# The opening of a fused attention and feed-forward kernel: first loads on two queues, both weight products before the keys, h1's copies on SyncE behind the keys

## The chip, the cores and the metric

One Trainium2 chip, one NeuronCore of it. The time is the device time of the whole program in microseconds (us), median of several runs. Engines are named as in the profile: PE is TensorE (PEld its weight loads), DVE is VectorE, ACT is ScalarE, POOL is GpSimd, SP is SyncE, which here issues DMAs only. ACT issues DMAs too, from the same instruction queue in which its activations stand.

## The reference

The input x has 2 batches of 2048 rows of 256 features, all in float32.

```python
xn = layernorm(x)                                   # over the 256 features, eps 1e-5
q, k, v = xn @ Wq, xn @ Wk, xn @ Wv                 # 256 -> 256
scores = where(causal, q @ k.T, -max) * 256 ** -0.5
attention = softmax(scores) @ v @ Wo
h = silu(tlin(xn, w1)) * tlin(xn, w2)               # 256 -> 1024; tlin(x, w) = (x @ w.T) * s
h = gelu(tlin(h, h1)); h = gelu(tlin(h, h2))        # 1024 -> 1024, exact gelu
return x + attention + tlin(h, w3)                  # 1024 -> 256
```

The entries of w1, w2, h1, h2 and w3 are -1, 0 or 1, each output feature with a scale s.

## The kernel before, in words

**Two parts.** The program first does all of attention, then the feed-forward part inside a branch (L1075): a flag, made during attention, tells whether the ternary weights have no low bits, and `ffn_ternary` (L692) runs then. Nothing of the feed-forward part starts before attention ends. It multiplies by h1 and h2 in seven products of quarters instead of eight, from sums of quarters that lie in the DRAM tensors `factors`.

**Numbers in two parts.** A float32 operand of a product is split into a high part, rounded for TensorE, and a low part, the rest. `hi_lo` (L207) does it: ACT copies the high part, DVE subtracts it. A product of two such operands is three matmuls: high by high, high by low, low by high. With the 256 features in two chunks this makes six matmuls of 512 columns.

**Weights.** Queries and keys never appear by themselves: `weights_product` (L212) makes wqk from Wq and Wk, so that a score is (xn wqk) xn, and wvo from Wv and Wo. What the code calls keys is the transposed, split xn; queries are xn times wqk, values xn times wvo.

**Blocks.** Rows come in blocks of 512 (TB), four a batch (NB), each of four tiles of 128 rows. Attention starts with the last block of the first batch, number 3. For each block, `start_keys` (L270) takes statistics on DVE (`stats`, L230), the root on ACT (`root`, L236) and normalises x in place on POOL (L278); `keys` (L288) transposes it on PE, splits it and stores it to DRAM (`xT_d`, L306, 1 MB a block, read again by the feed-forward part). `queries` (L308), `values` (L322) and `score` (L344) are PE's work on it. The second batch's keys are transposed by DVE in small squares and two passes through DRAM (`turn_blocks`, `fetch_blocks`), and so are the exponentials of most score rows: tile b goes to d in DRAM, and comes back as e. `turn` splits them (pT) and `weigh` (L429) multiplies them by the values.

**The opening** (L178 to L617): loads of x for blocks 3 to 0 on SP, of Wq and Wk on ACT; idle matmuls on PE (`WARM`); wqk; loads of Wv and Wo into the buffers that Wq and Wk leave; then keys, queries and one row of scores of block 3, wvo, and keys, scores and values of blocks 2 to 0.

**The loop after it** goes over 32 tiles of rows (j), and mixes the scores of tile j with the weighing of earlier tiles (`merged`, L43, by their numbers of columns). A tile is weighed no sooner than DELAY or DELAY_BLOCKS columns of PE work after its scores.

**Beside it**, from j = 3, `beside` (L595) counts PE's columns and each time a gap is full takes the next of a list of steps (`looks`): `fetched_weights` (L572) loads the next feed-forward weights on ACT's queue into two stg buffers; `low` and `odd` look at their bits on ACT and DVE; `sum_up` makes sums of h1's quarters on DVE and `store_sums` writes them to the DRAM tensor `factors["h1"]`; `copy_factors` (L538) fills the rest of it with three copies from DRAM to DRAM for each of four chunks, 256 KB each. At the end xh0 is loaded again (L690).

**Order on the engines.** Each engine works through its own list in order. The framework's scheduler builds these lists ahead of the run: it may put an instruction earlier than the text has it when its operands and its buffer are free. `tc.issue_after(ins)` puts what is made inside it behind `ins` on the engine of `ins`. The `marks` are the last such instructions: `marks["DVE"]` the last score row's copy, `marks["ACT"]` the last exponential. In the trace of before, the twelve copies of h1, which have no operand to wait for, are issued from ACT's queue between 1.7 and 19.6 us.

## Time and profile before

| what | value |
|---|---|
| time, median of 3 runs (lowest to highest) | 874.41 us (873.32 to 876.95) |
| the profiled execution's own time | 872.97 us |
| its span in the profile | 871.1 us |
| PE busy | 851.1 us (98%) |
| DVE, ACT, POOL busy | 630.3, 498.2, 236.3 us |
| DMA moved | 162.5 MB, 187 GB/s over the span |
| PE's first matmul of the feed-forward part | 278.16 us |
| mean granted PE clock | 0.993 |

Times inside the profile count from the start of its span; the profiled execution's own time is 1.9 us longer than the span. A row of a timeline gives start, duration, engine, line, operation and tiles (out from in), how many instructions were merged, and in brackets how long the engine was idle before it and what ended that. A row of a windows table gives the window, its length, busy time and instructions of PE, PEld, DVE, ACT and POOL, the granted PE clock, the DMA engines' busy share and GB/s. A row of waits gives engine and line, what it waited for, the sum in us, how many times, and the longest. A matmul's shown duration includes its way through the array, so that 512 columns show some 0.37 us while the next starts after 0.23; costs below are by such starts.

### The profile page before, as it was taken

To read this page: it belongs to the slowest core of one execution; us is meant where nothing else is said; L and a number is where in the kernel's file an instruction comes from. 1 tells how busy PE (TensorE), PEld (TensorE's weight loads), DVE (VectorE), ACT (ScalarE), POOL (GpSimd) and SP (SyncE) were. 2 spreads that over 40 slices of the span, in tenths; PEclk is the share of its full clock that TensorE was granted. 3 is DMA by queue.
4 is the path that set the end of the run, shared out by engine and by line. 5 is a ranking of instruction groups with operands and counts; after the bars stand their busy time and mean duration, and the time that the engine had idled before them with its cause. 6 is when DMAs were issued, how large, how long until landed. Compare 5 with 4: busy or idle time off the path is not lost.

```text
span 871.1 us, 12211 instructions
## 1 busy us (share of the span) xinstructions
PE 851.1 (98%) x4280; PEld 720.7 (83%) x4280; DVE 630.3 (72%) x1127; ACT 498.2 (57%) x881; POOL 236.3 (27%) x176
## 2 busy tenths in 40 slices
PE   8999999999989999999999999999999999999996
PEld 5888888988877878888988888988888898888886
DVE  5699688786873995985496596569478648848663
ACT  2547555755644665677266486536657635657670
POOL 4112633201111473540143150025024012402401
PEclk8999999999999999999999999999999999999999
DMA  9867599866792979743424444443444432144412
GB/s 322 312 230 226 176 326 300 298 230 212 243 324 93 375 280 336 273 146 143 139 87 150 146 144 145 149 127 103 145 145 145 146 139 97 49 145 146 145 49 77
DMA packets 63845, 162.51 MB, mean 187 GB/s; under 512 B 6560, under 2 KB 36384, under 8 KB 54560
## 3 DMA queue, kind: packets, MB, share of 16 engines
q1 hardware_dynamic: 58304, 145.92, 48.4%
q10 hardware_dynamic: 5472, 15.73, 5.6%
q8 instruction: 36, 0.59, 0.3%
q14 instruction: 33, 0.27, 0.1%
HBM read 120.21 MB, written 47.71 MB: 193 GB/s over the span
## 4 chain that ended last, share of the span: by engine, by line
PE 61%; DMA 3%; POOL 1%; DVE 1%; issue 0%; SPq 0%; DVEq 0%; POOLq 0%
PE ps_h_X L780 26%; PE ps_h_Z L780 13%; PE ps_w_B L736 10%; PE ps_h_Y L780 7%; PE ps_y L918 6%; DMA stgt_h<-in_ffn_h_w 1%; DMA w_h_S<-factors_h 1%; POOL sums_h L151 1%; DVE f_w_B L762 0%; DMA rt<-r_d 0%; POOL rt L908 0%; DVE h_B L720 0%; DMA out<-yt 0%; POOL f_w_B L761 0%; DVE f_w_B L742 0%
## 5 line engine op out<-in xcount | busy, mean ns | idle before, releaser
L359 PE MATMUL pss<-k,q 128*128 128x512 f32 (+3 forms) x480 | 110.4, 368 | 2.1 <-DVE q L210 1.1
L359 PEld LDWEIGHTS pss<-k,q 128*128 128x128 f32 x480 | 81.6, 189 | 14.9 <-DVE q L210 1.4
L780 PE MATMUL ps_h_X<-h_h_T,w_h_S 128*128 128x512 f32 x384 | 89.1, 389 | 0.3 <-DMA w_h_S<-factors_h 0.3
L780 PEld LDWEIGHTS ps_h_X<-h_h_T,w_h_S 128*128 128x128 f32 x384 | 72.0, 188 | 15.6 <-ACT k_h_u L801 0.7
L438 PE MATMUL po<-v,pT 128*128 128x512 f32 x272 | 79.0, 403 | 3.7 <-ACT pT L418 2.8
L420 POOL TENSOR_TENSOR pT<-e,pT 128x512 fp32r<-128x512 f32 (+3 forms) x30 | 35.6, 1188 | 161.6 <-ACT pT L418 111.0
L908 POOL TENSOR_TENSOR rt<-rt,xt 128x1024 f32<-128x1024 f32 x8 | 19.6, 2453 | 209.9 <-DMA rt<-r_d 209.9
L801 ACT ACTIVATE k_h_u<-k_h_u,h_s_sb 128x512 f32<-128x512 f32 x64 | 46.3, 724 | 41.1 <-DVE k_h_u L800 40.9
L741 ACT ACTIVATE f_w_B<-ps_w_B,w_s_sb 128x512 f32<-128x512 f32 x64 | 43.0, 684 | 43.5 <-PE ps_w_B L736 43.5
L918 PEld LDWEIGHTS ps_y<-w_sbt,h_h_B 128*128 128x128 f32 x512 | 62.0, 192 | 0.3
L918 PE MATMUL ps_y<-w_sbt,h_h_B 128*128 128x256 f32 x512 | 62.1, 283 | 0.0
L736 PE MATMUL ps_w_B<-xh,w_sb 128*128 128x512 f32 x256 | 59.5, 390 | 1.3 <-DVE r L457 1.3
L418 ACT CAST pT<-e 128x512 fp32r<-128x512 f32 (+3 forms) x60 | 32.6, 574 | 48.9 <-DMA e<-d 31.0
L780 PE MATMUL ps_h_X<-h_h_T,w_h_A 128*128 128x512 f32 x256 | 59.3, 389 | 0.0
L780 PE MATMUL ps_h_Y<-h_h_B,w_h_A 128*128 128x512 f32 x256 | 59.3, 389 | 0.0
L736 PE MATMUL ps_w_B<-xh1t,w_sb 128*128 128x512 f32 x256 | 58.7, 389 | 0.0
L438 PEld LDWEIGHTS po<-v,pT 128*128 128x128 f32 x272 | 48.6, 192 | 11.6 <-ACT pT L418 3.3
L736 PEld LDWEIGHTS ps_w_B<-xh,w_sb 128*128 128x128 f32 x256 | 47.8, 188 | 11.2 <-issue 1.5
L780 PEld LDWEIGHTS ps_h_Y<-h_h_B,w_h_A 128*128 128x128 f32 x256 | 48.0, 188 | 10.0
L780 PEld LDWEIGHTS ps_h_X<-h_h_T,w_h_A 128*128 128x128 f32 x256 | 48.0, 188 | 10.0
L736 PEld LDWEIGHTS ps_w_B<-xh1t,w_sb 128*128 128x128 f32 x256 | 48.0, 188 | 10.0
L380 ACT ACTIVATE s<-s,low 128x1024 f32<-128x1024 f32 (+7 forms) x48 | 43.0, 897 | 20.3 <-DVE low L374 19.9
(139 smaller groups left out, 1846.7 us busy)
## 6 DMA issues: line engine op xcount, KB each, us to landing
w_h_S<-factors_h SPq DMA_DIRECT2D x32, 1024.0 KB, 4.7
w_h_A<-factors_h SPq DMA_DIRECT2D x24, 1024.0 KB, 4.7
d<-b SPq DMA_DIRECT2D x18, 512.0 KB, 4.2
e<-d SPq DMA_DIRECT2D x72, 128.0 KB, 4.1
xT_d<-k SPq DMA_DIRECT2D x8, 1024.0 KB, 7.5
stg<-in_ffn_h_w ACTq DMA_DIRECT2D x16, 512.0 KB, 6.6
x<-in_attn_x SPq DMA_DIRECT2D x16, 256.0 KB, 5.5
r_d<-r SPq DMA_DIRECT2D x8, 512.0 KB, 5.3
```

What stands on the lines that cost most here:

```text
L151: engine.tensor_tensor(sums[:, i, :], x, y, op)
L359: nc.tensor.matmul(out=ps[:, :w], lhsT=qs[n][:, c, a, ts(t, P)], rhs=ks[m][:, c, b, :w], start=(k == 0), stop=(m < n and k == 3 * DC - 1),)
L380: marks["ACT"] = nc.scalar.activation(st["s"][:, at], st["s"][:, at], AF.Exp, bias=low, accum_out=st["sums"][:, u // UK : u // UK + 1],).ins
L418: nc.scalar.copy(hi, src)
L420: engine.tensor_tensor(lo, src, hi.bitcast(F32), ALU.subtract)
L438: nc.tensor.matmul(out=st["po"], lhsT=pT[:, 0, ts(j, P)], rhs=vs[m][:, j, :, :], start=(m == first and j == 0), stop=False,)
L736: nc.tensor.matmul(out=p, lhsT=w[:, c, ts(o, P)], rhs=xh[:, c, a, :], start=(c == 0 and a == 0), stop=(c == DC - 1 and a == 1),)
L741: nc.scalar.activation(f, p1, AF.Silu, scale=sc["w1"][:, o : o + 1])
L780: nc.tensor.matmul(out=out[o], lhsT=w[:, c, ts(o, P)], rhs=sets[right][c][:, a, :], start=(start and c == 0 and a == 0), stop=(c == HK - 1 ...
L801: nc.scalar.activation(C[k][o], r[o] if r else banks[o], AF.Gelu, scale=s[:, at : at + 1])
L908: nc.gpsimd.tensor_tensor(rest, rest, xt, ALU.add)
L918: nc.tensor.matmul(out=ys[t][:, :D], lhsT=h[c][:, a, ts(t, P)], rhs=w3_sb[:, c, :], start=(c == 0 and a == 0), stop=(c == HC - 1 and a == 1),)
```

## The change

- x of block 3 is fetched in two halves by SP and ACT. Wq and Wv go on SP's queue, Wk and Wo on ACT's, all ahead of blocks 2 to 0. Wv and Wo have a buffer of their own (a b buffer), so they wait for nothing.
- The idle matmuls have 256 columns instead of 512, and are 26 instead of 14; six more stand between keys and queries of block 3.
- Both weight products stand before the keys of block 3. Each has its matmuls in one PSUM tile, and its copies (`copied`) are made later: wqk's behind the keys, wvo's behind the scores of block 3 and queued behind the last high and low parts.
- Block 3's normalised x is made by POOL (tiles 0 and 2) and ACT (tiles 1 and 3). Statistics of blocks 2 to 0 are queued behind wqk's low part.
- Queries and scores do the six matmuls in another order: chunk inside, part outside.
- h1's copies go from ACT to SP, three behind each of the four xT_d stores of the first batch. The step of the list that held each triple is gone.
- Loads of feed-forward weights are queued behind the last exponential before them.

```diff
 TURN_KEYS = [8, 10, 12, 14]
 LOOKS_FROM = 3
 LEAD = 2
-WARM = 14
+WARM = 26
+WARM_KEYS = 6
...
         ps_o = actx.enter_context(tc.tile_pool(name="ps_o", bufs=2, space=PSUM))
         xs, rstds, ks, qs, vs = {}, {}, {}, {}, {}
-
-        def load_x(n):
+        marks = {}
+
+        def load_x(n, queues):
             t = xp.tile([P, NT, D], F32, tag="x", name=f"x_{n}")
-            for h in range(2):
+            for h, queue in enumerate(queues):
                 src = x[n // NB, ds((n % NB) * TB + h * 2 * P, 2 * P), :]
-                nc.sync.dma_start(out=t[:, ts(h, 2), :], in_=src.rearrange("(t p) d -> p t d", p=P))
+                queue.dma_start(out=t[:, ts(h, 2), :], in_=src.rearrange("(t p) d -> p t d", p=P))
             return t
-        xs[NB - 1] = load_x(NB - 1)
-        raw = {}
-        for name, src in (("q", wqT), ("k", wkT)):
-            raw[name] = stgp.tile([P, DC, D], F32, tag="stg", name=f"raw_{name}")
-            nc.scalar.dma_start(out=raw[name], in_=src)
+
+        xs[NB - 1] = load_x(NB - 1, (nc.sync, nc.scalar))
+        raw = {name: stgp.tile([P, DC, D], F32, tag="stg", name=f"raw_{name}") for name in "qk"}
+        both = bp.tile([P, 2, DC, D], F32, tag="b", name="raw_vo")
+        raw["v"], raw["o"] = both[:, 0], both[:, 1]
+        for name, src, queue in (
+            ("q", wqT, nc.sync), ("k", wkT, nc.scalar), ("v", wvT, nc.sync), ("o", wo, nc.scalar)
+        ):
+            queue.dma_start(out=raw[name], in_=src)
         nc.scalar.preload_act_table(AF.Sqrt)
         for n in range(NB - 2, -1, -1):
-            xs[n] = load_x(n)
+            xs[n] = load_x(n, (nc.sync, nc.sync))
         ident = cp.tile([P, P], F32, name="ident")
         make_identity(nc, ident)
...
         nc.gpsimd.memset(ones, 1.0)
-        idle = sp.tile([P, S], F32, tag="s", name="idle")[:, : TB // 2].bitcast(BF16)
+        idle = sp.tile([P, S], F32, tag="s", name="idle")[:, : TB // 4].bitcast(BF16)
         nc.vector.memset(idle, 0.0)
         ps_idle = ps_s.tile([P, TB], F32, tag="ps", name="ps_idle")
-        for _ in range(WARM):
-            nc.tensor.matmul(out=ps_idle, lhsT=idle[:, :P], rhs=idle, start=True, stop=True)
+
+        def keep_warm(k):
+            for _ in range(k):
+                nc.tensor.matmul(
+                    out=ps_idle[:, : TB // 2], lhsT=idle[:, :P], rhs=idle[:, : TB // 2], start=True, stop=True
+                )
+
+        keep_warm(WARM)
         def hi_lo(hi, lo, src):
-            nc.scalar.copy(hi, src)
-            nc.vector.tensor_tensor(lo, src, hi.bitcast(F32), ALU.subtract)
+            marks["hi"] = nc.scalar.copy(hi, src).ins
+            marks["lo"] = nc.vector.tensor_tensor(lo, src, hi.bitcast(F32), ALU.subtract).ins
         def weights_product(name, aT, b, factor):
             r = cp.tile([P, DC, 2, D], F32R, name=name)
+            ps = ps_s.tile([P, DC, D], F32, tag="ps", name=f"ps_{name}")
             for c in range(DC):
-                ps = ps_s.tile([P, TB], F32, tag="ps", name=f"ps_{name}_{c}")
                 for d in range(DC):
                     nc.tensor.matmul(
-                        out=ps[:, :D], lhsT=aT[:, d, ts(c, P)], rhs=b[:, d, :],
+                        out=ps[:, c, :], lhsT=aT[:, d, ts(c, P)], rhs=b[:, d, :],
                         start=(d == 0), stop=(d == DC - 1),
                     )
-                f = rp.tile([P, D], F32, tag="y", name=f"wf_{name}_{c}")
-                nc.scalar.mul(f, ps[:, :D], factor)
-                nc.vector.tensor_copy(r[:, c, 0, :], f)
-                nc.vector.tensor_tensor(
-                    r[:, c, 1, :], f, r[:, c, 0, :].bitcast(F32), ALU.subtract
-                )
-            return r
+
+            def copied():
+                f = rp.tile([P, NT, D], F32, tag="r", name=f"wf_{name}")[:, :DC, :]
+                nc.scalar.mul(f, ps, factor)
+                nc.vector.tensor_copy(r[:, :, 0, :], f)
+                marks["lo"] = nc.vector.tensor_tensor(
+                    r[:, :, 1, :], f, r[:, :, 0, :].bitcast(F32), ALU.subtract
+                ).ins
+
+            return r, copied
         def stats(xt, mv, n):
             for t in range(NT):
...
             xt = xs.pop(n)
             if n not in rstds:
                 mv = cp.tile([P, NT, 2], F32, name=f"mv_{n}")
-                stats(xt, mv, n)
+                with ExitStack() as behind:
+                    if n < NB - 1:
+                        behind.enter_context(tc.issue_after(first_lo))
+                    stats(xt, mv, n)
                 rstds[n] = root(mv, NT, str(n))
             rstd, off = rstds[n]
             for t in range(NT):
+                if n == NB - 1 and t % 2:
+                    nc.scalar.activation(
+                        xt[:, t, :], xt[:, t, :], AF.Identity,
+                        scale=rstd[:, t : t + 1], bias=off[:, t : t + 1],
+                    )
+                    continue
                 nc.gpsimd.tensor_scalar(
                     xt[:, t, :], xt[:, t, :], rstd[:, t : t + 1], off[:, t : t + 1],
                     ALU.mult, ALU.add,
...
                 for t in range(NT):
                     nc.tensor.transpose(pt[:, ts(t, P)], xn[:, t, ts(c, P)], ident)
                 hi_lo(ks[n][:, c, 0, :], ks[n][:, c, 1, :], pt)
-            nc.sync.dma_start(out=xT_d[n], in_=ks[n].bitcast(F32).rearrange("p c h t -> p (c h t)"))
+            marks["SP"] = nc.sync.dma_start(out=xT_d[n], in_=ks[n].bitcast(F32).rearrange("p c h t -> p (c h t)")).ins
         def queries(n, m):
             if m == 0:
                 qs[n] = qp.tile([P, DC, 2, TB], F32R, tag="q", name=f"q_{n}")
             pp = ps_s.tile([P, TB], F32, tag="ps", name=f"pq_{n}_{m}")
             k = 0
-            for c in range(DC):
-                for a, b in ((0, 0), (0, 1), (1, 0)):
+            for a, b in ((0, 0), (1, 0), (0, 1)):
+                for c in range(DC):
                     nc.tensor.matmul(
                         out=pp, lhsT=wqk[:, c, a, ts(m, P)], rhs=ks[n][:, c, b, :],
                         start=(k == 0), stop=(k == 3 * DC - 1),
...
             at = (m - first) * TB
             ps = ps_s.tile([P, TB], F32, tag="ps", name=f"pss_{n}_{t}_{m}")
             k = 0
-            for c in range(DC):
-                for a, b in ((0, 0), (0, 1), (1, 0)):
+            for a, b in ((0, 0), (0, 1), (1, 0)):
+                for c in range(DC):
                     nc.tensor.matmul(
                         out=ps[:, :w], lhsT=qs[n][:, c, a, ts(t, P)], rhs=ks[m][:, c, b, :w],
                         start=(k == 0), stop=(m < n and k == 3 * DC - 1),
...
             nc.sync.dma_start(out=f[:, 1:5, c, :], in_=sums.bitcast(F32))
         def copy_factors(src, f, c):
-            nc.scalar.dma_start(out=f[:, 0, c, :], in_=src[:, c, :HB])
-            for i in range(2):
-                nc.scalar.dma_start(out=f[:, 5 + i, c, :], in_=src[:, c + HK, ts(i, HB)])
+            with tc.issue_after(marks["SP"]):
+                nc.sync.dma_start(out=f[:, 0, c, :], in_=src[:, c, :HB])
+                for i in range(2):
+                    nc.sync.dma_start(out=f[:, 5 + i, c, :], in_=src[:, c + HK, ts(i, HB)])
         def item_low(src, dst):
             items.append(([src], [(0, lambda t: low(t, dst))]))
...
                 (1500, lambda t: store_sums(f, c)),
                 (1500, lambda t: odd(t[0])),
                 (3000, lambda t: odd(t[1])),
-                (3000, lambda t: copy_factors(src, f, c)),
             ]
             items.append(([src[:, c, :], src[:, c + HK, :]], steps))
-        for src, dst in ((w1, w1_sb), (w2, w2_sb)):
-            for c in range(src.shape[1]):
-                item_low(src[:, c, :], dst[:, c, :])
+        for c in range(HK):
+            src, dst = ((w1, w1_sb), (w2, w2_sb))[c // DC]
+            item_low(src[:, c % DC, :], dst[:, c % DC, :])
         w3_at = list(range(0, HC, SC // D))
         for c in range(HK):
             item_factors(h1, factors["h1"], c)
...
         def fetched_weights(i):
             for src in items[i][0]:
                 t = stgp.tile([P, SC], F32, tag="stg", name=f"stg_{i}_{len(tiles_of[i])}")
-                nc.scalar.dma_start(out=t, in_=src)
+                with tc.issue_after(marks["ACT"]):
+                    nc.scalar.dma_start(out=t, in_=src)
                 tiles_of[i].append(t)
...
                     looks.pop(0)[1]()
-        wqk = weights_product("wqk", raw["q"], raw["k"], scale)
-        for name, src in (("v", wvT), ("o", wo)):
-            raw[name] = stgp.tile([P, DC, D], F32, tag="stg", name=f"raw_{name}")
-            nc.scalar.dma_start(out=raw[name], in_=src)
+        wqk, wqk_copied = weights_product("wqk", raw["q"], raw["k"], scale)
+        wvo, wvo_copied = weights_product("wvo", raw["v"], raw["o"], 1.0)
         keys(NB - 1)
+        wqk_copied()
+        first_lo = marks["lo"]
+        keep_warm(WARM_KEYS)
         queries(NB - 1, 0)
         queries(NB - 1, 1)
         order = list(range(NB - 1, -1, -1))
         score(NB - 1, NT - 1, NB - 1, order)
-        wvo = weights_product("wvo", raw["v"], raw["o"], 1.0)
+        with tc.issue_after(marks["hi"]), tc.issue_after(marks["lo"]):
+            wvo_copied()
+        copy_factors(h1, factors["h1"], 0)
         for n in order[1:]:
             keys(n)
+            copy_factors(h1, factors["h1"], NB - 1 - n)
             score(NB - 1, NT - 1, n, order)
             for half in range(2):
                 values(n + 1, half)
...
         def before(j):
             if 3 <= j < 3 + NB:
                 n = NB + j - 3
-                x1 = xs[n] = load_x(n)
+                x1 = xs[n] = load_x(n, (nc.sync, nc.sync))
                 with tc.issue_after(marks["DVE"]):
                     stats(x1, mv1[:, j - 3], n)
             if j == 3 + NB:
```

## The prediction

> **What bounds the kernel now.** I read the page's engine line first, then the busy time by windows, then the timeline of the first 30 us, then TensorE's waits.
>
> ```profile
> span 871.1 us, 12211 instructions
> PE 851.1 (98%) x4280; PEld 720.7 (83%) x4280; DVE 630.3 (72%) x1127; ACT 498.2 (57%) x881; POOL 236.3 (27%) x176
> ```
>
> ```profile
> 0.00:10.00 10.00, 7.22 (x25) 3.54 (x26) 4.34 (x20) 2.24 (x4) 2.93 (x15) 1.00 0.86 289
> 10.00:20.00 10.00, 9.20 (x31) 6.48 (x31) 7.53 (x30) 3.00 (x7) 5.72 (x11) 0.66 1.00 350
> ...
> 50.00:60.00 10.00, 10.00 (x52) 8.52 (x51) 10.00 (x27) 6.15 (x13) 2.59 (x2) 1.00 0.70 227
> ...
> 340.00:856.00 516.00, 516.00 (x2489) 436.42 (x2487) 362.62 (x510) 309.31 (x522) 127.31 (x68) 1.00 0.39 137
> ```
>
> TensorE (PE) is the bound: 98% busy, and without a gap from 340 to 856 us. Time can be won only where PE waits, runs at a low clock or does idle work. In the window lines the order is PE, PEld, DVE, ACT, POOL, clock, DMA share, GB/s: the first 20 us hold 56 matmuls, and the clock averages 0.66 in the second ten. The start is the weak place, and DMA is full there (share 1.00).
>
> ```profile
> 4.76 0.75 DVE L233 BATCH_NORM_STATS2 st<-x 128x6 f32<-128x256 f32 x2 [3.62 <-DMA x<-in_attn_x]
> ...
> 6.20 0.75 DVE L233 BATCH_NORM_STATS2 st<-x 128x6 f32<-128x256 f32 x2 [0.48 <-DMA x<-in_attn_x]
> ...
> 7.57 0.75 DVE L233 BATCH_NORM_STATS2 st<-x 128x6 f32<-128x256 f32 x2 [0.39 <-DMA x<-in_attn_x]
> ...
> 8.77 2.22 POOL L278 TENSOR_SCALAR x<-x,rstd,off 128x256 f32<-128x256 f32 x4 [6.50 <-DVE off L242]
> ...
> 9.38 2.09 PE L304 MATMUL ptx<-ident,x 128*128 128x128 f32 x8 [1.49 <-POOL x L278]
> ...
> 12.04 5.82 PE L315 MATMUL pq<-k,wqk 128*128 128x512 f32 x12 [0.57 <-ACT k L209]
> ...
> 18.97 1.03 PE L218 MATMUL ps_wvo<-raw_o,raw_v 128*128 128x256 f32 x4
> ...
> 23.24 2.96 PE L331 MATMUL pv<-wvo,k 128*128 128x256 f32 x24
> ```
>
> This is the opening chain: x of block 3 lands in two halves (4.76 and 6.20), statistics, the normalised x one tile after the other on POOL, transposes in step with them, then twelve query matmuls in 5.82 us. The third line is the next block's statistics, standing on VectorE (DVE) ahead of block 3's reciprocal (8.32).
>
> ```profile
> 4.90:8.20 3.30, 2.99 (x14) 1.91 (x12) 2.43 (x10) 0.30 (x1) 0.00 (x0) 1.00 1.08 387
> 8.30:11.60 3.30, 1.75 (x8) 0.81 (x8) 3.00 (x17) 0.86 (x3) 2.22 (x4) 1.00 1.08 394
> 11.70:15.00 3.30, 2.96 (x6) 1.98 (x7) 3.30 (x13) 1.27 (x4) 0.21 (x1) 0.50 1.08 382
> 15.10:18.40 3.30, 3.30 (x12) 2.61 (x10) 1.49 (x8) 1.09 (x2) 3.30 (x7) 0.50 0.85 270
> 18.50:22.00 3.50, 3.50 (x20) 2.98 (x19) 1.85 (x5) 0.77 (x3) 3.02 (x6) 1.00 1.00 368
> ```
>
> ```profile
> PE po L438 <- ACT pT L418: 2.8, 1, 2.8
> ```
>
> After the thin stretch 8.3 to 11.6 (eight matmuls) the clock is halved for 6.8 us, over all the queries. The last line, of TensorE's waits, is its longest after that, at 258 us, where e's blocks land late.
>
> **What the Trainium skill says.** "TensorE: Matmul & The Clock Gate", Part 1: activity is judged over free-running windows of about 3.4 us, and an idle one halves the clock. The trace agrees: two such windows at 0.50. "DMA: Bandwidth & Descriptors", Issuing engines are not separate DMA queues: queues share the 16 engines, and a second one saves issue time only. The trace agrees: Wq on ScalarE's (ACT's) queue and x's first half on SP's land at 4.2 and 4.7, their successors at 5.6 and 6.2. "ScalarE: Activation LUTs", Table sets: identity is in every table set, so x normalised on ACT should need no table load; no Identity runs in the trace of before.
>
> **The change, part by part.**
>
> *Loads.* DMA moves about 0.387 MB/us when full. By 4.7 us it has brought Wq and x's first half, 0.5 MB; the change puts both halves of x there, so x is whole at about 4.75 instead of 6.2. Wq and Wk (another 0.5 MB, 1.35 us) land near 6.1 instead of 4.2 and 5.6, Wv and Wo near 7.5 instead of 13.5 and 14.9. Block 2 lands near 8.9 as now: h1's copies no longer share, but Wv and Wo are ahead.
>
> *Statistics to keys.* Two tiles of statistics take 0.97 us (4.76 to 5.73), so four end at 6.7; root on ACT 0.3 and its handover 0.1, reciprocal and offset 0.3 plus 0.1: ready at 7.5 instead of 8.66. Of the 1.15 us, 0.75 is the next block's statistics, which the change holds behind wqk's low part. Normalising: POOL takes 0.55 a tile, two tiles end at 8.7; ACT's two, at some 0.4 (nearest row: L223, 128x256, 0.38), at 8.4. Before: 10.99. On PE, though, wqk starts at 6.3 instead of 6.0 and takes 8 x 0.216 = 1.7, to 8.0; wvo needs the same 1.7, to 9.75; if it stands first, the eight transposes (8 x 0.11 warm) start only then. The first key cast starts at about 10.45 instead of 11.40: **0.95 us**. If the transposes stand ahead of wvo it is 1.7 us; if Wv comes late, nothing. I take the middle one.
>
> *Clock.* PE is now busy from 1.2 to 9.75 nearly without a gap, then transposes, then six idle matmuls of 256 columns (6 x 0.11 = 0.65, laid into the 0.73 us that PE waits between transposes and queries now). So no window is idle. The queries cost 12 x 0.23 = 2.76 plus about 0.25 for low parts instead of 5.6 (12.04 to 17.66): **2.6 us**. The 26 short warm-up matmuls end where 14 long ones did: 17 cold at 0.21, nine warm at 0.11, from 1.19 to 5.8.
>
> *wvo.* Its eight matmuls (2 x 1.03 us in the timeline, 8 x 0.216 start to start) now stand at 19 to 21.8 in a dense stretch; before the keys they fill a wait: **1.7 us**. Its copies become two of double width on ACT and DVE; wqk's too; DVE's total stays about 2.5 us.
>
> *Statistics of blocks 2 to 0* (3 x 2 us on DVE) were done in DVE's free time from 7.6 to 15.9 and now start after about 10.2. DVE then has, to the end of the opening, these 6, key, query and value low parts and wvo 11, row copies 2.8: about 20 us, against 19.5 us of PE work (24 transposes 2.6, four scores 5.6, four blocks of values 11.2). Close, so PE will wait here and there: after the queries (0.6 us for q's low parts), before block 1's keys (0.5). Before had about 1.4 us of waits from 18 to 40. Taken as +0.3; bounds: -2 (DVE last) to +1.
>
> *h1's copies*: twelve DMAs of 256 KB. They leave ACT's queue (8 x 0.56 and 4 x 0.5 us of issuing, with waits for earlier landings in between) and go to SP, three behind each xT_d store. On SP they pass the loads of the second batch's x and stand before the first block transposes (d from b, 43.5 us now). Bytes to be moved before that: x 2, weights 1, copies 3, xT_d 4, second x 2 = 12 MB, 32 us at the full rate; about 34 us, while the first d store comes due at about 38. They are read only at 282 us. Cost zero; the cover is DELAY_BLOCKS, 42000 columns or 18.6 us between a score and its weighing.
>
> *Weight loads behind an Exp.* Two of the 22 leave 21.9 us for about 63; w1 is first masked at 70.7, after a landing of 4 to 6 us. The others stay about where they are. Nothing taken.
>
> *Steps.* Four empty steps of 3000 columns go: 3000/512 x 0.227 = 1.33 us each, so the last item ends 5.3 us earlier against PE. Its loads (240.7, 242.9, 251.9) and xh's reload (241.7, 1 MB) stand in front of e's blocks that land at 260.3 instead of near 256, which is the 2.8 us wait and a further 1.2 us at half clock. Earlier loads relieve this, and crowd another place. Other waits between 120 and 215 (1.2, 1.7, 1.1 us) hang on the same items. Bounds -3 to +5; I take **+0.9**.
>
> *Order of the six matmuls* in queries and scores: count unchanged; a fresh tile waits less for its low part, 0 to 0.3 us. In the sum at nothing; the cover is PE's dense queue.
>
> Sum: 0.95 + 2.6 + 1.7 + 0.3 + 0.9 = 6.4 us off the profiled 872.97 us: 866.5. That execution is 1.4 us under the median of 874.41, so the median becomes **868.0**.
>
> **Rivals.** *Late relief too*: the 258 us wait goes whole (4 us instead of 0.9): 864.9. For it: its cause is transfers that move; against: others take their place. *A thin start*: the clock still drops once, or DVE's delayed statistics hold the keys of blocks 2 to 0; either costs 2 to 3 us: 871.0. For it: DVE's 20 us against PE's 19.5. *The built order differs from the text*, so that the copies or wvo stand elsewhere: also about 871. *Slower*: weight loads block ACT. Each waits in ACT's queue until its buffer is free, now 1.33 us sooner after the DVE step that frees it, and pinned behind an Exp; exponentials, casts of pT and all of PE's weighing queue behind. At 123 us such a pair (DVE L525, then a load) already stands beside 2.7 us of idle ACT and 1.2 us of PE. Over 22 loads, 0.25 us each eats the opening's 5.5 us; at 0.5 us each the net is +5: 879. Against: PE has blocks of slack there, and most loads already stand in those places.
>
> **Numbers.** The forecast 0.58 (own range 865.5 to 870.5), late relief 0.15, thin start or other order 0.17, blocked ACT 0.10. A measurement of this kernel tells about 0.5%, 4.4 us, from no change: under 870.0 counts as faster. Forecast gives 0.53 of it, relief 0.15, thin start 0.02: 0.70. Within: 0.05 + 0.15 + 0.02 = 0.22. Slower: 0.08. The range 863.5 to 872.5 leaves out blocked ACT and the tails of relief and thin start.
>
> **What would show it.** Right: statistics without a pause from about 4.75; queries beginning near 11 and taking about 3 us at clock 1.00; values of block 3 near 17 instead of 23.2; the first exponential near 35.5 instead of 40.95; FFN's first matmul near 272 instead of 278.2. Wrong: clock 0.50 between 9 and 19; DVE solid with PE waiting from 12 to 33; ACT idle at each weight load from 70 to 260; a first d store later than 40.

## The result: 0.7% slower, and the profile after

The changed kernel takes 879.62 us (median of 8, 877.06 to 881.58), the kernel before 873.29 beside it (869.03 to 876.95). The ratio is 1.0072, with a 95% interval of 1.0051 to 1.0092: slower, by 6.3 us. The prediction was 868.0. The profiled execution took 880.16 us, its span 878.3; the sum had given 866.5 for the one of before.

First the page of the changed kernel, its span and engine line:

```profile
span 878.3 us, 12241 instructions
...
PE 852.5 (97%) x4298; PEld 721.7 (82%) x4298; DVE 627.7 (71%) x1123; ACT 498.8 (57%) x881; POOL 233.5 (27%) x174
```

TensorE (PE) is busy 1.4 us longer than before and waits 5.8 us more (878.3 - 852.5 = 25.8 against 20.0). The busy time by windows of the changed kernel (columns as before: PE, PEld, DVE, ACT, POOL, granted clock, DMA share, GB/s):

```profile
0.00:10.00 10.00, 8.95 (x48) 7.18 (x49) 2.99 (x13) 3.27 (x5) 2.78 (x14) 1.00 0.82 281
10.00:20.00 10.00, 8.82 (x49) 6.34 (x47) 10.00 (x39) 4.39 (x10) 3.43 (x7) 1.00 0.85 276
...
11.70:15.00 3.30, 3.16 (x12) 1.88 (x12) 3.30 (x17) 0.93 (x3) 0.00 (x0) 1.00 0.61 202
15.10:18.40 3.30, 2.87 (x15) 2.02 (x15) 3.30 (x13) 1.92 (x6) 2.17 (x4) 1.00 0.95 299
...
36.98:281.46 244.48, 233.52 (x1271) 199.76 (x1270) 187.16 (x477) 137.66 (x271) 60.34 (x58) 0.99 0.74 239
```

The clock is 1.00 where it was 0.50: that part came. New is DVE: 10.00 of the second ten microseconds. The last line runs from the first score behind the opening to the feed-forward part's (FFN's) first matmul. Before, the same stage took 237.92 us (40.24 to 278.16). So the opening won 3.3 us, and the stage behind it, where the change hardly touches anything, lost 6.6.

The timeline of the changed kernel's opening:

```profile
4.12 0.75 DVE L249 BATCH_NORM_STATS2 st<-x 128x6 f32<-128x256 f32 x2 [3.12 <-DMA x<-in_attn_x]
...
6.72 1.10 POOL L303 TENSOR_SCALAR x<-x,rstd,off 128x256 f32<-128x256 f32 x2 [4.47 <-DVE off L258]
8.34 1.89 PE L231 MATMUL ps_wvo<-raw_vo 128*128 128x256 f32 x8
...
9.17 0.43 DVE L239 CAST wqk<-wf_wqk 128x512 fp32r<-128x512 f32 x1 [2.56 <-ACT wf_wqk L238]
...
10.07 1.04 PE L329 MATMUL ptx<-ident,x 128*128 128x128 f32 x8
10.24 1.40 DVE L249 BATCH_NORM_STATS2 st<-x 128x6 f32<-128x256 f32 x4
...
11.56 3.30 PE L340 MATMUL pq<-k,wqk 128*128 128x512 f32 x12 [0.46 <-ACT k L222]
```

The queries run in 3.30 us instead of 5.82. But DVE is idle for 2.56 us ahead of 9.17. Up to 8.63, when the first half of block 2 lands, it has nothing to measure; from there the statistics could start, but they may not pass wqk's low part (this is called the hold below). They start at 10.24, 1.6 us behind the landing, and DVE is full until 20 us.

Then the place where the lead goes. ACT's timeline in the changed kernel, with PE's next matmuls:

```profile
77.08 0.60 ACT L442 CAST pT<-e 128x512 fp32r<-128x512 f32 x1
77.21 0.33 ACTq L600 DMA_DIRECT2D stg<-in_ffn_w_w  x1
82.94 0.62 ACT L442 CAST pT<-e 128x512 fp32r<-128x512 f32 x1 [5.25 <-DMA e<-d]
...
84.99 1.14 ACT L404 ACTIVATE s<-s,low 128x1024 f32<-128x1024 f32 x1
...
89.53 0.73 PE L462 MATMUL po<-v,pT 128*128 128x512 f32 x2 [2.62 <-ACT pT L442]
```

ACT issues a weight load of 512 KB at 77.21, and its next instruction is a cast that waits for e's blocks until 82.94. The four parts of that e were issued by SP from 74.72 to 76.8. In the kernel before, the same cast waited for nothing:

```profile
78.84 0.34 ACTq L575 DMA_DIRECT2D stg<-in_ffn_w_w  x1
...
80.42 0.61 ACT L418 CAST pT<-e 128x512 fp32r<-128x512 f32 x1
```

Compared matmul by matmul, the changed kernel is 3.3 us ahead from 38 to 86 us. Behind the wait at 89.5 and one stretch at half clock (90.64 to 94.05) it is 1.2 us late, at the FFN's first matmul 3.3 (281.46), at the last matmul 3.7, at the span's end 7.2. The last 3.5 us are the tail, from the last matmul to the end of the span: 10.7 us against 7.1.

TensorE's waits in the changed kernel, whole span:

```profile
PE po L462 <- ACT pT L442: 5.7, 6, 2.6
PE pf L715 <- DVE most L713: 1.7, 1, 1.7
```

The 2.8 us wait at 258 us has two successors at 261 to 264, of 1.7 (a matmul of the flag, which stands in PE's list ahead of the weighing) and 0.8 us. Little was relieved there.

### The profile page after: what moved, and what is told of

The parts are those of the page before. It is cut to its first block, busy times and chain, and to the rows that moved or that the text cites. A ratio compares the mean times of both kernels' runs of the same rounds, so it can differ in the third digit from the quotient of the medians.

```text
span 878.3 us, 12241 instructions
## 1 busy us (share of the span) xinstructions
PE 852.5 (97%) x4298; PEld 721.7 (82%) x4298; DVE 627.7 (71%) x1123; ACT 498.8 (57%) x881; POOL 233.5 (27%) x174
## 4 chain that ended last, share of the span: by engine, by line
PE 74%; DMA 11%; DVE 6%; ACT 3%; issue 2%; SPq 2%; POOL 1%; DVEq 0%; ACTq 0%; POOLq 0%
PE ps_h_X L809 26%; PE ps_w_B L765 13%; PE ps_h_Z L809 12%; PE ps_h_Y L809 7%; PE ps_y L947 6%; DMA e<-d 6%; PE pss L383 2%; PE po L462 2%; DMA stg<-in_ffn_h_w 2%; SPq L278 2%; PE pv L356 1%; DVE s L392 1%; PE po L467 1%; DMA w_h_S<-factors_h 1%; DVE xh L153 1%
## 5 line engine op out<-in xcount | busy, mean ns | idle before, releaser
L462 PE MATMUL po<-v,pT 128*128 128x512 f32 x272 | 81.2, 408 | 5.7 <-ACT pT L442 5.7
L770 ACT ACTIVATE f_w_B<-ps_w_B,w_s_sb 128x512 f32<-128x512 f32 x64 | 42.9, 683 | 43.7 <-PE ps_w_B L765 43.6
L765 PEld LDWEIGHTS ps_w_B<-xh1t,w_sb 128*128 128x128 f32 x256 | 48.0, 188 | 10.2 <-issue 0.2
L790 POOL TENSOR_TENSOR k_h_u<-k_h_p,k_h_u 128x512 f32<-128x512 f32 x16 | 24.3, 1523 | 110.0 <-ACT h_h_B L748 97.6
```

Source lines behind the costliest of these rows:

```text
L462: nc.tensor.matmul(out=st["po"], lhsT=pT[:, 0, ts(j, P)], rhs=vs[m][:, j, :, :], start=(m == first and j == 0), stop=False,)
L765: nc.tensor.matmul(out=p, lhsT=w[:, c, ts(o, P)], rhs=xh[:, c, a, :], start=(c == 0 and a == 0), stop=(c == DC - 1 and a == 1),)
L770: nc.scalar.activation(f, p1, AF.Silu, scale=sc["w1"][:, o : o + 1])
L790: nc.gpsimd.tensor_tensor(B["B12"][i], B["B22"][i], B["B12"][i], ALU.subtract)
```

## The experiments

Seventeen kernels, each timed in five rounds beside the kernel before. Ratios are to the kernel before, with 95% intervals; 0.001 is 0.87 us. *Exp*: first exponential. *FFN*: its first matmul. *Fetch*: for the sixth fetch of e (the one that the cast above waits for), from the issue of its last part to its landing. *Load*: how long after that issue the next weight load was issued. *Tail*: last matmul to the span's end. The last five columns come from one profile each, in us.

| kernel | ratio | Exp | FFN | Fetch | Load | Tail |
|---|---|---|---|---|---|---|
| before | 1 | 41.0 | 278.2 | 3.0 | 1.8 | 7.1 |
| after | 1.0072 (1.0051 to 1.0092) | 37.7 | 281.5 | 6.0 | 0.4 | 10.7 |
| opening | 1.0122 (1.0092 to 1.0152) | 43.6 | 289.2 | 5.7 | 0.2 | 8.1 |
| rest | 1.0006 (0.9989 to 1.0022) | 38.6 | 277.7 | 3.2 | 2.8 | 7.6 |
| a_unpinned | 1.0092 (1.0061 to 1.0124) | 39.7 | 285.1 | 6.0 | 0.3 | 9.3 |
| a_steps | 1.0089 (1.0060 to 1.0117) | 37.6 | 283.5 | 4.9 | 0.3 | 9.9 |
| late_load | 1.0040 (1.0028 to 1.0053) | 38.3 | 281.4 | 2.9 | 3.3 | 7.8 |
| late_stats | 1.0094 (1.0060 to 1.0128) | 37.2 | 289.3 | 2.4 | 2.1 | 8.3 |
| idle16 | 1.0068 (1.0046 to 1.0089) | 36.7 | 285.7 | 2.4 | 4.4 | 7.4 |
| tail | 1.0023 (1.0012 to 1.0034) | 37.6 | 283.6 | 5.5 | 0.6 | 5.5 |
| a_order | 1.0024 (1.0010 to 1.0038) | 37.1 | 279.2 | 2.8 | 1.9 | 10.3 |
| a_wvo | 1.0073 (1.0048 to 1.0099) | 38.6 | 284.1 | 5.7 | 0.3 | 10.0 |
| a_stats | 1.0013 (0.9998 to 1.0028) | 35.4 | 275.1 | 3.2 | 3.7 | 10.2 |
| b_tail | 0.9972 (0.9959 to 0.9986) | 39.6 | 276.8 | 3.2 | 1.6 | 5.5 |
| stats_tail | 0.9961 (0.9944 to 0.9978) | 35.8 | 279.9 | 3.2 | 3.7 | 5.4 |
| stats_order_tail | 0.9993 (0.9976 to 1.0009) | 36.6 | 277.2 | 3.2 | 0.7 | 5.4 |
| exp_first | 1.0053 (1.0036 to 1.0070) | 38.1 | 282.7 | 6.0 | 0.5 | 9.5 |
| b_hold | 1.0066 (1.0041 to 1.0092) | 40.4 | 283.3 | 6.1 | 0.5 | 7.5 |
| b_hold_late | 1.0044 (1.0028 to 1.0059) | 42.1 | 282.1 | 3.1 | 3.2 | 7.7 |

Attention is the same program in tail as in after, and still its FFN starts 2.1 us later; b_tail has the attention of before and starts it 1.4 us sooner, stats_tail that of a_stats and 4.8 us later. A single profile tells a place, and the medians tell the time.

### Which half of the change: opening and rest

opening is the changed kernel with h1's copies and the loads as before; rest is the kernel before with only the copies on SP, the step removed and the weight loads queued behind an exponential (called pins below).

```diff
 # opening, against the changed kernel
-            with tc.issue_after(marks["SP"]):
-                nc.sync.dma_start(out=f[:, 0, c, :], in_=src[:, c, :HB])
+            nc.scalar.dma_start(out=f[:, 0, c, :], in_=src[:, c, :HB])
...
+                (3000, lambda t: copy_factors(src, f, c)),
...
-                with tc.issue_after(marks["ACT"]):
-                    nc.scalar.dma_start(out=t, in_=src)
+                nc.scalar.dma_start(out=t, in_=src)
 # rest is the reverse of these edits, in the kernel before
```

> The changed kernel with h1's copies put back on ScalarE's queue and into the list of steps, and the weight loads no longer pinned behind an Exp; loads of x and of the attention weights, both products, x normalised by two engines and the order of matmuls as in the changed kernel. Theory 1 (the opening's lead is lost where a weight load meets e's blocks on the DMA engines, because ScalarE's list there has the load directly ahead of a cast that waits for e): the lead at 40 us is 1 to 3 us, smaller than the changed kernel's 3.3 since the copies crowd the loads; the wait of 2.6 us at about 87 us and the half clock behind it are there; time 1 to 3 us over before. Theory 2 (the pinned loads and the removed steps cost it): no wait at 87 us, time 3 to 6 us under before.

> The kernel before with only h1's copies on SyncE behind the keys' stores, their step gone from the list, and the weight loads pinned behind an Exp. Theory 1: the wait at 87 us is not there, since without the opening's lead the lists of ScalarE keep the order of before in that place; time within 3 us of before. Theory 2: slower by 4 to 9 us, with waits of TensorE beside the weight loads between 80 and 265 us.

rest costs nothing: copies on SP, step and pins are neutral together. At the first exponential it is even 2.4 us ahead, of which up to 1.7 may be the clock (one stretch of 3.41 us at half clock in its opening, 6.83 us in the kernel before); it has handed all but 0.6 back by 90 us. opening is the slow half, and by 10.7 us, more than either expectation. It is late in its own opening (43.6 against 41.0): h1's copies stand in ACT's list there again, and PE waits 1.9 and 3.0 us for ACT's casts of k and q. It loses more behind it.

### The two edits of the loop: a_unpinned and a_steps

```diff
 # a_unpinned
-                with tc.issue_after(marks["ACT"]):
-                    nc.scalar.dma_start(out=t, in_=src)
+                nc.scalar.dma_start(out=t, in_=src)
 # a_steps
                 (3000, lambda t: odd(t[1])),
+                (3000, lambda t: None),
```

> The changed kernel, weight loads not pinned behind an Exp. Theory 1: only the first two loads move (53 to about 20 us); the load at 77 us and the wait at 87 us stay; time within 1.5 us of the changed kernel. Theory 2: 4 us or more come back.

> The changed kernel with an empty step of 3000 columns where each triple of copies stood in the list. Theory 1: nothing before 110 us changes, so the wait at 87 us stays; waits after 110 us move; time within 2 us of the changed kernel. Theory 2 (the missing steps bring loads and sums too close): the waits after 110 us shrink and 2 to 4 us come back.

Neither recovers anything, so the pins and the removed steps are not the cause. Both still have the slow fetch (6.0 and 4.9 us).

### Is the lead worth anything: idle16

```diff
                 values(n + 1, half)
+        ps_pad = ps_s.tile([P, TB], F32, tag="ps", name="ps_pad")
+        for _ in range(16):
+            nc.tensor.matmul(
+                out=ps_pad, lhsT=wqk[:, 0, 0, :P], rhs=ks[0][:, 0, 0, :], start=True, stop=True
+            )
```

> The changed kernel, with 16 idle matmuls of 512 columns (3.6 us of TensorE) at the end of the opening, before the second score tile. If TensorE's lead of 3.3 us is slack that is handed back at the wait near 87 us: that wait (2.8 us) and the half clock behind it (1.7 us) go, and the time is 0 to 2 us under 879.6. If the lead is real time and the wait at 87 us is of another origin (the collision of a load with e), the wait stays or moves with the matmuls, and the time is 2 to 4 us over: 882 to 883.5.

3.6 us of idle PE work, and the ratio stays what it was (1.0068 against 1.0072; 3.6 us more would be 1.0113). So, by the median, PE's lead behind the opening buys little in the changed kernel. This is not clean: the slow fetch is gone here too (2.4 us), and late_load below puts some 2.8 us on that, which could pay for most of the idle work. In place of the wait near 87 us one of 1.7 us stands at 92 us, for POOL's low part. And the lead is not all of the loss: at 46 us this kernel stands where the kernel before does (0.5 us later), and it begins its FFN 7.5 us later.

### The meeting of a load with e: late_load, exp_first, late_stats

late_load moves the load of 77.21 us behind the cast that waits for e. exp_first leaves the load and moves that cast behind the exponential that stood behind it. late_stats takes DVE work out of 50 to 73 us.

```diff
 # late_load
-                nc.scalar.copy(hi, src)
+                cast = nc.scalar.copy(hi, src).ins
+                if (n, t, m) == (3, 1, 2):
+                    with tc.issue_after(cast):
+                        fetched_weights(3)
...
 # exp_first
+                    if (n, t, m) == (3, 1, 2):
+                        behind.enter_context(tc.issue_after(marks["ACT"]))
                     nc.scalar.copy(hi, src)
 # late_stats
+            if 6 <= j < 6 + NB:
+                n = NB + j - 6
                 with tc.issue_after(marks["DVE"]):
-                    stats(x1, mv1[:, j - 3], n)
+                    stats(xs[n], mv1[:, j - 6], n)
...
-TURN_KEYS = [8, 10, 12, 14]
+TURN_KEYS = [10, 11, 12, 14]
```

> The changed kernel, with one 512 KB weight load (the one issued at 77.21 us, 0.4 us behind the last part of a fetch of e) put behind ACT's cast of that e. Collision theory: the load made e land at 82.83 instead of about 79.9, and ACT, whose next cast waits for e, stood for 5.25 us with an exponential behind it; so e lands near 80, the wait at 87 us (2.8 us) falls below 1 us, the clock stays 1.00 from 90 to 94, the lead of 3.3 us over the kernel before is still at least 2 us at 100 us, and the time is 3 to 5 us under the changed kernel's 879.6. Rival, VectorE sets the pace (full from 44 to 80 us, so that e's blocks come no sooner than before): the wait only moves to the next e, the lead is gone by 100 us all the same, and the time is within 1.5 us of the changed kernel's.

> The changed kernel, with one cast of ACT (the one that stood 5.25 us for a late e at 77.7 to 82.9 us) put behind the exponential that followed it in ACT's list. If standing in a list behind a late transfer is what costs: that exponential runs near 80 us instead of 85, its d is stored near 82 instead of 87.5, the later wait near 87 to 94 us falls by 2 us or more, half clock there gone, ratio 1.003 to 1.005. If the lead goes in any list (VectorE and transfers set the pace): ratio 1.006 to 1.008, and other waits between 95 and 160 us grow by what this one loses.

> The changed kernel, with the statistics of the second batch's x (4 times about 2 us of VectorE, pinned at score tiles 3 to 6, some 50 to 73 us) moved to tiles 6 to 9, their root and the turning of keys behind them. VectorE theory: the store of d that stands at 74.2 us comes near 71.5, e lands before the weight load starts, the wait at 87 us falls below 1 us, the time is 3 us under 879.6. Collision theory: ACT's list still puts the load beside a fetch of e; a wait of 2 us or more stays between 83 and 93 us, and the time is within 1.5 us of 879.6 (later statistics may cost up to 2 us more at the keys of the second batch).

In late_load the fetch takes 2.9 us, the wait is 0.3, and the clock is not halved before the last matmul. ACT's timeline and PE's matmul there:

```profile
81.26 0.62 ACT L442 CAST pT<-e 128x512 fp32r<-128x512 f32 x1 [2.25 <-DMA e<-d]
81.59 0.38 ACTq L603 DMA_DIRECT2D stg<-in_ffn_w_w  x1
...
87.85 0.73 PE L465 MATMUL po<-v,pT 128*128 128x512 f32 x2 [0.31 <-ACT pT L442]
```

The time falls by 2.8 us (1.0072 to 1.0040). Each theory has half: moving the load was worth about that much, and the lead is gone all the same, at waits of 1.0 us near 106 and 1.7 near 143. Two things weaken it. The lists of ACT, DVE and PE differ from the changed kernel's in many more places behind 77 us, and in this one profile the FFN starts where it did (281.4), while the tail is shorter (7.8 us instead of 10.7). b_hold_late below is the cleaner case. A store of d was issued 1.0 us behind this fetch and did it no harm. exp_first has the slow fetch still (6.0 us), but its exponential runs at 82.23 instead of 84.99 and no wait over 1 us stands between 80 and 100. At 1.0053 it lies between the two expectations, and against 1.0072 its interval decides nothing; waits for DVE of 1.5 us and less at 138 to 152 us took their share. late_stats too loses the wait near 87 us, but PE then waits 2.6 us in one place near 139 us for the second batch's keys, which it made late: no gain, and nothing said on DVE's pace.

Why a load that ACT issues delays a fetch that SP issues is in the Trainium skill, "DMA: Bandwidth & Descriptors", Issuing engines are not separate DMA queues: DMAs of different engines "will ultimately run on the same 16 DMA engines and interleave with each other". The table agrees. Where the load follows within 0.2 to 0.6 us, the fetch takes 4.9 to 6.1 us (eight profiles); elsewhere 2.4 to 3.3 (the other eleven, the nearest load at 0.7). Such a meeting need not cost anything, though. In the kernel before the next fetch of e stands behind a load of 80.55 us and lands 6.3 us after its last issue. ACT waits for it as well, and PE waits for nothing from 84 to 96 us:

```profile
89.59 1.15 ACT L418 CAST pT<-e 128x512 fp32r<-128x512 f32 x2 [3.46 <-DMA e<-d]
```

### Which part of the opening: a_stats, a_order, a_wvo

```diff
 # a_stats
-                    if n < NB - 1:
+                    if n < 0:
                         behind.enter_context(tc.issue_after(first_lo))
 # a_order, in queries and score
-            for a, b in ((0, 0), (0, 1), (1, 0)):
-                for c in range(DC):
+            for c in range(DC):
+                for a, b in ((0, 0), (0, 1), (1, 0)):
 # a_wvo: this line now stands behind the first score tile
         wvo, wvo_copied = weights_product("wvo", raw["v"], raw["o"], 1.0)
```

> The changed kernel, without holding the statistics of blocks 2 to 0 behind wqk's low part. The opening loses up to 1 us (VectorE does another block's statistics first). If the held statistics carry the slower middle stage (their 6 us of VectorE moved from 8 to 16 us to behind 10 us, and its queue is full from there on): ratio 1.003 or less, the middle stage 240 us or less. If not: 1.006 to 1.010.

> The changed kernel, with the six matmuls of queries and scores in the order of the kernel before. Found so far: the stage from the first score after the opening to the FFN takes 237.9 us before, 239.5 in rest, but 244 to 246 in every kernel with the new opening, whatever its lead there. Theory that one part of the change carries this, here the order of matmuls (it stands in that stage, and rest does not have it): ratio to before 1.002 or less, the stage 240 us or less. Rival, the stage is slower because each engine's list, built from the opening's timing, meets the transfers of d and e in another order, whichever part caused it: the ratio stays between 1.005 and 1.010, the stage at 243 or more.

> The changed kernel, with the product of Wv and Wo behind the first score tile, as in the kernel before (its loads stay early). The product then costs 1.7 us in a dense stretch, and the transposes of block 3 stand 1.7 us sooner. If wvo ahead of the keys is the part that carries the slower middle stage: ratio 1.003 or less. If it is worth what the opening shows: 0 to 1.5 us slower than the changed kernel, ratio 1.007 to 1.009. If the lead is worthless in any case: 1.005 to 1.008, the changed kernel's own 1.0072.

a_stats is the find: not holding the statistics takes 5.2 us off. Its DVE timeline, where the hold had left DVE idle, and its first exponential:

```profile
8.29 0.76 DVE L249 BATCH_NORM_STATS2 st<-x 128x6 f32<-128x256 f32 x2 [1.32 <-DMA x<-in_attn_x]
...
35.44 1.15 ACT L404 ACTIVATE s<-s,low 128x1024 f32<-128x1024 f32 x1
```

Block 2 is measured as soon as it has landed, and the first exponential comes at 35.44: the opening that had been predicted for the changed kernel. In the waits of PE from 11.6 to 38 us, the changed kernel has 1.1 us before scores for k and 0.4 for q; a_stats has neither. The profiles bear this out: in a_stats and stats_tail the first exponential comes at 35.4 and 35.8, in the six that have this opening with the hold (after, a_steps, late_load, late_stats, tail, exp_first) at 37.2 to 38.3. And the fetch of a_stats is early (last part issued at 73.2), ahead of the load at 76.8.

a_wvo: no difference that its interval shows (which leaves room for 2 us), although its first exponential is 0.9 us later. So wvo ahead of the keys was worth about that in the opening, and nothing of it shows at the end. a_order regains 4.2 us by itself, with its FFN at 279.2, and the fetch clear of the load. It still has the hold, so what the hold costs depends on the lists around it.

### Is the hold the cause by itself: b_hold and b_hold_late

b_hold puts that one edit into the kernel before. b_hold_late moves one load in it, as in late_load.

```diff
 # b_hold, against the kernel before
+                with ExitStack() as behind:
+                    if n < NB - 1:
+                        behind.enter_context(tc.issue_after(lows["wqk"]))
                     stats(xt, mv, n)
```

> The kernel before, with the one edit that its statistics of blocks 2 to 0 are held behind wqk's low part, as the change does. If holding them costs by itself (VectorE idle ahead of 10 us, full behind it): first exponential 1 to 3 us later than 40.95, ratio 1.002 to 1.007. If it costs only in the new opening, where VectorE has less room: within 0.002 of 1.

> b_hold (1.0066), with the weight load that is issued 0.5 us behind the last part of a fetch of e put behind ACT's cast of that e, as in late_load. In eight profiles such a load starts 0.2 to 0.6 us behind the fetch, and the fetch takes 4.9 to 6.1 us; in the ten others it starts elsewhere, and the same fetch takes 2.4 to 3.3 us. If that meeting carries the loss of the held statistics: that fetch takes about 3 us again, no wait over 1 us and no half clock between 85 and 96 us, ratio 1.003 or less. If it is one of several, and the lead it saves is taken at the next wait, as in late_load: ratio 1.003 to 1.005. If the loss has another place: 1.005 or more.

The hold alone makes the kernel before as slow as the whole change does: 1.0066. In its profile the first exponential is not late (40.36 against 40.95), but there the clock hides the cost. The second ten microseconds in b_hold, in b_hold_late, which has the same opening, and in b_tail, which has that of before:

```profile
10.00:20.00 10.00, 8.02 (x36) 5.82 (x37) 8.33 (x35) 3.19 (x8) 4.47 (x9) 1.00 0.99 321
```

```profile
10.00:20.00 10.00, 8.68 (x32) 6.46 (x33) 8.22 (x33) 2.70 (x6) 4.42 (x9) 0.83 0.99 350
```

```profile
10.00:20.00 10.00, 8.99 (x37) 6.46 (x36) 7.35 (x30) 2.95 (x8) 6.15 (x12) 0.83 1.00 340
```

b_hold met no half clock there (1.00), the kernel before much of it (0.66). b_hold_late and b_tail met the same (0.83), and of these two the one with the hold has its first exponential 2.5 us later: 42.09 against 39.56. One pair of profiles says that the hold costs the old opening about what it costs the new one.

More is lost behind the opening, at the same cast: 3.9 us against the kernel before from 88 to 95 us. The timelines of ACT and PE in b_hold:

```profile
79.35 0.33 ACTq L580 DMA_DIRECT2D stg<-in_ffn_w_w  x1
85.00 0.63 ACT L423 CAST pT<-e 128x512 fp32r<-128x512 f32 x1 [5.16 <-DMA e<-d]
...
91.59 0.73 PE L443 MATMUL po<-v,pT 128*128 128x512 f32 x2 [2.01 <-ACT pT L423]
```

ACT's timeline in b_hold_late, where of all ACT's list only that load and that cast change places:

```profile
83.71 0.62 ACT L423 CAST pT<-e 128x512 fp32r<-128x512 f32 x1 [2.16 <-DMA e<-d]
83.79 0.33 ACTq L583 DMA_DIRECT2D stg<-in_ffn_w_w  x1
```

The same five microseconds in windows, b_hold and then b_hold_late:

```profile
90.00:95.00 5.00, 3.41 (x11) 2.77 (x12) 2.28 (x6) 2.56 (x7) 3.38 (x5) 0.73 0.56 178
```

```profile
90.00:95.00 5.00, 5.00 (x28) 4.27 (x28) 2.19 (x5) 1.39 (x3) 5.00 (x8) 1.00 0.59 199
```

PE is busy for 3.41 of them in b_hold and for all 5 in b_hold_late. The wait, the half clock (0.73 to 1.00) and the slow fetch (6.1 to 3.1 us) go, and the ratio falls to 1.0044. That is 1.9 us; the two intervals overlap, so the size is uncertain, but it is near late_load's 2.8. The load is one part of the hold's loss. The rest, some 3.8 us, goes with a list of waits that no single edit here removed.

### The tail: tail and b_tail

```diff
-                rest = op.tile([P, NT, D], F32, tag="r", name=f"rt_{m}", bufs=1)
-                nc.sync.dma_start(out=rest, in_=r_d[m].rearrange("p (t d) -> p t d", d=D))
...
-                nc.gpsimd.tensor_tensor(rest, rest, xt, ALU.add)
+                rests = []
+                for i in range(2):
+                    rest = op.tile([P, 2, D], F32, tag=f"r{i}", name=f"rt_{m}_{i}", bufs=1)
+                    nc.sync.dma_start(
+                        out=rest, in_=r_d[m].rearrange("p (t d) -> p t d", d=D)[:, ts(i, 2), :]
+                    )
+                    nc.gpsimd.tensor_tensor(rest, rest, xt[:, ts(i, 2), :], ALU.add)
+                    rests.append(rest)
```

> The changed kernel, with the residual rows of the FFN's output in two tiles of half size, so that the first half's reload is issued about 4 us sooner and its addition on POOL takes half as long. In the profile of the changed kernel the last reload took 4.56 us (3.33 before) and the outputs behind it 3.7 to 4 us (1.7 before). If the tail is that reload: from the last matmul to the span's end 6 to 7.5 us instead of 10.7, FFN's first matmul where it is (within 1 us of 281.5), time 3 to 4 us under 879.6. If the tail's DMAs are slow by themselves, wherever the reload stands: at least 9.5 us there, and no more than 1 us gained.

> The kernel before, with the residual rows in two tiles of half size, as in tail (which took the changed kernel from 1.0072 to 1.0023). If the changed kernel's tail is slow beyond that of before (10.7 against 7.1 us from the last matmul to the span's end), the same edit gains less here: 1 to 2 us, ratio 0.998 to 0.999, and then 2.5 to 3.5 us of the loss of 6.3 lie in the tail. If both tails are alike in the median and that profile was only an unlucky one: the same 4.3 us here, ratio 0.995, and the tail has no part in the loss.

The end of the changed kernel, behind its last matmul's operands: SP's reload of the residual rows, POOL's addition, the last outputs.

```profile
861.28 0.44 SPq L934 DMA_DIRECT2D rt<-r_d  x1
...
866.00 2.38 POOL L937 TENSOR_TENSOR rt<-rt,xt 128x1024 f32<-128x1024 f32 x1 [46.62 <-DMA rt<-r_d]
868.42 1.10 DVE L954 TENSOR_TENSOR yt<-yt,rt 128x256 f32<-128x256 f32 x3 [2.24 <-POOL rt L937]
868.87 5.32 SPq L955 DMA_DIRECT2D out<-yt  x4
```

The reload can start only when its buffer is free (861.28), takes 4.6 us, and the addition 2.4 more; the outputs then take 3.7 to 4 us each where the kernel before has 1.7. With two halves the changed kernel wins 4.3 us, the kernel before 2.4, between its two expectations. Both gain, the changed one by 1.8 more, though the intervals of the two gains overlap: by the medians about 2 us of its loss would lie in the tail, by the profiles 3.5. What goes with slow outputs are packets of 16 KB that fetch instructions on the same DMA engines. Take the four outputs ahead of the last one in all 19 profiles: the 14 that had no such packet in their time took 1.7 to 1.8 us, and all 44 that took over 2.6 us had one. In the changed kernel one starts at 870.71, amid three outputs, in the kernel before at 866.36, when they are nearly done. Every profile has such packets in its last 16 us, and no run moved them: a coincidence in time, and not a cause that is shown.

### The two together: stats_tail and stats_order_tail

stats_tail is a_stats with the edit of tail; stats_order_tail has the edit of a_order as well.

> a_stats (the changed kernel, statistics of blocks 2 to 0 not held) with the residual rows in halves as in tail. a_stats stood at 1.0013 although its FFN began at 275.1 us, 3.0 sooner than in the kernel before, because 10.2 us lie between its last matmul and the span's end (7.1 before). If the loss that is left in a_stats is the tail: ratio 0.995 to 0.998, tail 5.5 us, FFN near 275. If the early FFN in that profile was one lucky execution: ratio 0.999 or more.

> stats_tail with the six matmuls of queries and scores in the order of the kernel before as well. a_stats alone regained 5.2 us and a_order alone 4.2 us of the changed kernel's 6.3. If each of the two carries a loss of its own: they add up, ratio 0.990 to 0.994. If what both do is only to reshuffle the engines' lists and the meeting of transfers behind the opening: no sum, ratio within 0.003 of stats_tail, either side.

stats_tail takes 872.06 us beside 874.64, ratio 0.9961: faster than both kernels, and level with b_tail (0.9972) within the intervals. So even with the hold gone the opening's gain does not show beside the same tail edit without it. In its profile a wait of PE and two stretches of half clock stand between 138 and 147 us. stats_order_tail is 2.8 us slower than stats_tail (0.9993; the two intervals just touch): a_stats and a_order do not add up. The old order of the six matmuls won 4.2 us beside the hold and lost 2.8 us without it, so it has no fixed price. It moves the lists behind the opening, and in a_order that went with a fetch clear of the load; that this is its whole effect is not shown.

## Why the prediction was wrong

**The step that failed** is *Statistics of blocks 2 to 0*, +0.3 us with bounds -2 to +1. In the opening alone the hold cost 2.2 us (first exponential 37.67 with it, 35.44 without): the bound, not the value. DVE's amount of work was right (20.0 us busy from 10.2 to 38 us). The sum did not ask when it comes: block 2's statistics wait from 8.63 to 10.24, DVE is then full until 20 us, and the keys come late, for which PE waits 1.1 us. At the end the hold cost 5.2 us by a_stats, 5.8 in the kernel before by b_hold, and for what it does behind the opening the sum had no term at all. That price is not fixed: a_order regained 4.2 us with the hold in place.

**The sum's silent step** was that a microsecond of PE won in the opening is one at the end. 3.3 us were won (first exponential 40.95 to 37.67), and 6.6 lost in the stage behind. With the hold gone it is the same: stats_tail's first exponential comes 3.8 us ahead of b_tail's (35.8 against 39.6), and the medians differ by 1 us, within the intervals. idle16 points the same way, less cleanly. The prediction did say that PE has "blocks of slack" there, and used it only against the slower rival.

**Term by term.**
- *Loads*: x whole at 4.4 (predicted 4.75), Wq and Wk at 5.7 (6.1), Wv and Wo at 8.0 (7.5), block 2 at 9.4 (8.9). Right within 0.6 us.
- *Statistics to keys*: 0.47 instead of 0.95 (first key cast 11.40 to 10.93). wqk began at 6.61, not 6.3, and wvo ended at 10.07, with the transposes behind it as assumed.
- *Clock*: the clock stayed at 1.00; queries 3.30 us instead of 5.82, predicted 2.6 saved, 2.5 measured. But this compares with one profile that had two windows at half clock. b_tail, which has the same opening, and rest had one, so the usual saving is smaller. And the stretch ahead of the half clock had not been idle: PE was busy for 1.75 of its 3.30 us.
- *Normalising on ACT*: without a table load, as assumed (none between 2.27 and 36.37 us).
- *wvo*: 1.7 predicted, 0.9 in the opening (a_wvo) and nothing at the end.
- *h1's copies* at nothing: right (rest, 1.0006).
- *Weight loads behind an Exp* at nothing: right for the pins (a_unpinned), though the first two loads went to 53.2 us and not to 63. Not seen was that a load may fall beside a fetch of e.
- *Steps*, +0.9: wrong. The end of the list still costs 2.5 us at 261 us, and putting a step back changes nothing that the intervals show.
- *Order of six matmuls* at nothing: no fixed price (4.2 us lost beside the hold, 2.8 won without it).
- The tail was no term; about 2 us of the loss lie there.

**The rivals.** The slower rival gave 879, the measured time, and named weight loads and ACT. That its number fits is luck, for its way was another: loads that wait for their buffer in ACT's queue, 22 times. What the runs show is one load that does not wait at all, but shares the DMA engines with the fetch that ACT's next instruction needs. *A thin start* had "DVE's delayed statistics hold the keys of blocks 2 to 0", at 2 to 3 us: that mechanism came with that size, but it was counted only as far as the opening goes. Two signs of being wrong came in part: DVE solid, from 10 to 20 us, and a first store of d just later than 40 (40.22).

**What stays open.** Some 3.8 us of b_hold's loss and the corresponding waits of the changed kernel between 95 and 265 us have no single place: each experiment that removes one wait has others, and the lists of ACT, DVE and PE change wherever the opening does. To give the changed kernel the lists of the kernel before was not tried.

## What to carry to other kernels

A lead of the busiest engine is not yet a gain at the end: before adding it, follow the chain that feeds the next stage (here exponential, turning on DVE, store of d, fetch of e, cast) to the first wait behind the edit. Ask for a pin not only what it protects but when the held work then comes: the first of the held statistics started 1.6 us late, DVE was then full for ten microseconds, and without the hold the kernel took 5.2 us less. And where an engine both issues bulk loads and waits for small fetches in one list, look at each load that starts within a microsecond of a fetch.

## What was not expected of the hardware

- A fetch of four parts of 96 KB took 2.4 to 3.3 us from its last issue to its landing by itself, and 4.9 to 6.1 us when a 512 KB load was issued 0.2 to 0.6 us behind it. A load 0.7 us or more behind, or a store of 512 KB 1.0 us behind, left it at 2.4 to 3.3.
- The changes of the granted clock lie on a grid of 3.41 us, fixed within an execution and elsewhere in each. "TensorE: Matmul & The Clock Gate", Part 1, has such windows run freely and lets an idle one halve the clock; here a window that was idle by half was enough. Of the windows at full clock from 5 us to the last matmul, in all 19 profiles, 22 had PE idle for over 1.72 us, and half clock followed each. Of 34 with 1.30 to 1.72 us it followed 7, and none of the 4697 with less. (The ends of matmuls are modelled, so these limits are rough.) What a wait costs thus depends on where it falls. The wait of 2.0 us in b_hold lies in one window, and the next is at 0.50:

```profile
88.86:92.27 3.41, 1.40 (x8) 0.88 (x7) 2.32 (x7) 3.40 (x7) 0.65 (x1) 1.00 0.68 269
92.28:95.69 3.41, 3.41 (x12) 2.71 (x11) 0.69 (x1) 0.30 (x1) 3.41 (x7) 0.50 0.47 99
```

The wait of 2.5 us in a_wvo lies across two, 1.3 us in one and 1.2 in the other, and the clock stays at 1.00:

```profile
85.68:89.09 3.41, 2.12 (x13) 1.51 (x11) 1.78 (x3) 3.38 (x9) 0.00 (x0) 1.00 0.50 159
89.09:92.51 3.42, 2.21 (x12) 1.85 (x13) 2.28 (x6) 2.20 (x6) 2.18 (x3) 1.00 0.48 183
...
90.30:97.00 6.70, 6.70 (x38) 5.65 (x39) 2.19 (x7) 2.17 (x5) 6.67 (x11) 1.00 0.25 62
```

- Of the last outputs of 128 KB, three took 1.7 to 1.8 us each in the kernel before and 3.7 to 4.0 in the changed one, with the same instructions there; in rest and b_hold two took 4 us as well. The slow ones all had a packet of instructions of 16 KB in their time.
